# Merged and centred projections, a one-pass gate, and scans handed out in quarter steps in a four-layer image network on one Trainium2 core

## The chip, the core and the metric

The kernel runs on one NeuronCore of a Trainium2 chip. Its engines work side by side, each through its own list of instructions in order: TensorE (PE, matrix products into PSUM), VectorE (DVE, elementwise work and scans), ScalarE (ACT, functions such as the exponential), GpSimd (POOL) and SyncE (SP), which here issues the transfers. The metric is the time on the device in microseconds, the median of several executions. Everything is computed in fp32.

## The reference

Eight images of 256 channels and 32 x 32 pixels (1024 tokens) pass through four layers, each `x = x + layer(group_norm(x))`:

- layer 0: attention with 8 heads of 64, with normalised q and k, then a projection (`wout`);
- layers 1 and 2: a 3x3 convolution of 256 to 256 channels each;
- layer 3: a mixer, of which the change touches nearly every part:

```python
xn = layernorm(xs)                      # over channels, then split in 4 branches of 64
u, z = split(xs @ inw.T)                # per branch, 128 wide each
u = silu(causal depthwise conv of 4 taps (u))
xdbc = u @ xpw.T                        # 4 + 16 + 16 values: dt, B, C
dt = softplus(xdbc[..., :4] @ dtw.T + dtb)
y = selective_scan(u, dt, B, C, -exp(alog), dp)   # h = exp(dt*A)*h + dt*u*B; y = sum(h*C)
xm = y * silu(z) @ outw.T + skip * xc
Q = conv1x1(grouped conv of 3 taps (x_concat, 4 groups)); g = sigmoid(Q); xg = g * xm
R = conv1x1(depthwise3(xg)) + xg
xm2 = conv1x1(depthwise3(concat(xs, R))) + xs
x_local = depthwise3(xm2)
x_global = mha(xm2) = softmax(q k / sqrt(32)) v @ outw.T + outb    # 8 heads of 32
x_out = concat(x_local, x_global) @ fc_w.T + fc_b
x_out = gelu(layernorm(x_out)); xi = ln_hw(x_out)
xi = depthwise 3x3 (xi); x_mixed = layernorm(xi) @ proj_w.T + proj_b
```

## The kernel before, in words

A token row of 1024 values lies along the free dimension, channels on the 128 partitions, so an activation is two tiles of 128 x 1024. A projection from 256 to 256 channels is 2 x 2 x 2 matmuls of 128 x 128 x 512. The profile shows each fp32 matmul as two records.

**Two streams.** For one image the work is cut into `front_attention`, `front_convs` (layers 0 to 2), `scan_layers` (the four branches with their scans), then `back_layers` (gate, the convolutions of layer 3, its attention), `back_out` (the projections `aout` and `fcw`) and `back_end` (layer norm, GELU, 3x3 taps, layer norm, `projw`). The last loop of `preact_stack` (lines 1363 to 1400) works on three images at once: while the scans of image b run, the *dense* stream does the back of image b-1 and the front of image b+1. All are generators. A dense piece yields a cost; `interleave` adds these up and takes one step of the scans for each `PACE[b]` of cost (1.8 for the first image, 2.95, and 1.6 for the last). What is left of the scans is done at the end. `amid` (line 1348) puts pieces of `back_end` among the pieces of `front_convs`, at numbered places; `slow` counts the costs of the front's attention at 0.35. The order on each engine follows this order of issue: the wrapper `Paced` (line 93, whose line 101 is the line of nearly all instructions in the profile) ties each scan instruction to come after the dense instruction issued before it on the same engine, and blocks under `urgent` come early.

**The scans.** `scan_steps` (line 885) has 64 units an image: 4 branches x 2 halves of 512 tokens x 4 quarters of the states x 2 pairs of groups. A unit loads `dt`, `du` and `bc` from DRAM, ScalarE makes two decays `exp(dt*a)` into the two `da` buffers of PSUM, GpSimd makes the drives (`drive`, line 931), DVE scans twice (`tensor_tensor_scan`), GpSimd weighs the result (`weigh`, line 963) and PE sums it over states (`add_up`, into `y`). Before the change a unit takes two steps: both decays, then both scans with `weigh`, `drive` and `add_up`. `branch_front` prepares a branch in six pieces: the product with `minw` into `raw`, the taps and tanh into `u`, the product with `mxpw` into `low` (4 + 16 + 16 rows), then from rows 32 to 35 of `low` the product with `mdtw` and the softplus, then the stores of `dt` and `du`. `branch_back` ends a branch in two pieces. Both take `da` buffers for their products, and `scan_layers` puts their pieces between the steps of the scans.

**The back.** The gate in `back_layers` is a convolution of three taps from 256 to 4 rows: for each tap and channel tile a matmul with 4 columns of weights (12 in all), a copy by ScalarE to `q4`, then a product with `qpr` and a tanh. Attention in layer 3 (`mixer_attention`) leaves its unnormalised output in `o`; the sums go to DRAM and back, are inverted, spread by DMA into `rs`, and `finish` multiplies `o` by `rs` and adds the bias of v. `back_out` projects `o` with `aout` to `glob` and then `local` and `glob` with `fcw` to `xo`, which goes to DRAM; `back_end` loads it again and starts with `layer_norm` (line 293): mean over channels by a matmul with `mean_w`, subtraction, squares, variance, scale.

Of the kernel before, what the change touches and what calls it, by code (L numbers as in the profile page):

```python
# [11 lines left out]
F32 = mybir.dt.float32  # L12
# [21 lines left out]
def preact_stack(ctx: ExitStack, tc: tile.TileContext, I, out, cols):  # L34
# [25 lines left out]
    dp = ctx.enter_context(tc.tile_pool(name="dp", bufs=2, space=DRAM))  # L60
    xdp = ctx.enter_context(tc.tile_pool(name="xdp", bufs=3, space=DRAM))
# [87 lines left out]
    def chunk(name, i):  # L149

        src = I[name]
        k, n = src.shape[2:]
        t = wsp.tile([P, HALF], F32, tag="w", name="w")
        t = t[:, 0 : k * n].rearrange("p (k n) -> p k n", n=n)
        nc.sync.dma_start(out=t, in_=src[i])
        return t
# [4 lines left out]
    mdtw = wp.tile([36, NB, P], F32, name="mdtw")  # L161
    nc.sync.dma_start(out=mdtw[32:36], in_=I["mdtw"])
    qpw = wp.tile([NB, NB], F32, name="qpw")
    nc.sync.dma_start(out=qpw, in_=I["qpw"])
    qdwb = wp.tile([NB, 1], F32, name="qdwb")
    nc.sync.dma_start(out=qdwb, in_=I["qdwb"])
# [25 lines left out]
    qdw = wp.tile([P, 2, 3, NB], F32, name="qdw")  # L192
# [5 lines left out]
    qpr = wp.tile([NB, NB, 64], F32, name="qpr")  # L198
    vector.tensor_copy(qpr, qpw.unsqueeze(2).to_broadcast([NB, NB, 64]))
# [13 lines left out]
    vector.tensor_scalar_mul(qdw, qdw, 2.0)  # L213
    half_d = wp.tile([P, NB], F32, name="half_d")
# [9 lines left out]
    for t in images + [raw]:  # L224
        nc.gpsimd.memset(t, 0.0)

# [66 lines left out]
    def layer_norm(ts, sq, parts, small, finish):  # L293


        for tok, psum in parts:
            pm = psum()
# [418 lines left out]
    def conv3x3(xt, mv, name, bname, evac):  # L716
# [10 lines left out]
        for m in range(2):  # L727
            ps = big_tile()
            n = 0
            for c in range(2):  # L730
                for dy in range(3):
# [11 lines left out]
                    if n < 18:  # L743
                        yield 5.2
            evac(m, ps)
            channel_stats(mv, m, xt[:, m])
            yield 5.2
# [36 lines left out]
    def branch_front(i, xn, br):  # L784
# [3 lines left out]
        for h in range(2):  # L788
            ps = da_tile()
            tensor.matmul(  # L790
                ps,
                minw[rows, j, 0:P],
                inner(xn[j])[rows, HALVES[h]],
                start=True,
                stop=True,
            )
            scalar.copy(raw[:, 3 + h * HALF : 3 + (h + 1) * HALF], ps)
        yield
        u = mp.tile([P, N], F32, tag="u", name="u", bufs=2)
        uu = u[:, 0:N]  # L800
        scalar.activation(
            uu,
            raw[:, 3 : 3 + N],
            AF.Identity,
            bias=col("convb", i),
            scale=col("convw", 4 * i + 3),
        )
        for k in range(3):
            vector.scalar_tensor_tensor(
                uu, raw[:, k : k + N], col("convw", 4 * i + k), uu, ALU.mult, ALU.add  # L810
            )
        th = raw[:, 3 : 3 + N]
        scalar.activation(th, uu, AF.Tanh, scale=0.5)
        vector.scalar_tensor_tensor(uu, th, 1.0, uu, ALU.add, ALU.mult)
        br["u"] = u
        yield

        low = mwork("low")
        for h in range(2):
            ps = da_tile()  # L820
            tensor.matmul(
                ps[0:36], mxpw[:, i], u[:, HALVES[h]], start=True, stop=True
            )
            scalar.copy(low[0:36, HALVES[h]], ps[0:36])
        br["bc"] = dp.tile([DS, 2, 2, HALF], F32, tag="bc", name="bc")
        for k in range(2):
# [3 lines left out]
            )  # L830
        yield

        a, dt = mwork("a"), mwork("dt")
        aa, ee, dd = a[:, 0:N], raw[:, 3 : 3 + N], dt[:, 0:N]
        for h in range(2):
            ps = da_tile()
            tensor.matmul(
                ps, mdtw[32:36, i], low[32:36, HALVES[h]], start=True, stop=True  # L840
            )
            vector.tensor_scalar_add(a[:, HALVES[h]], ps, col("dtb", i))
        scalar.activation(ee, aa, AF.Abs)
        scalar.activation(ee, ee, AF.Exp, scale=-1.0)
        yield
        vector.tensor_scalar_add(dd, ee, 1.0)
        vector.scalar_tensor_tensor(ee, dd, -1.0, ee, ALU.add, ALU.subtract)
        scalar.activation(dd, dd, AF.Ln)
        vector.tensor_sub(dd, dd, ee)
        vector.scalar_tensor_tensor(dd, aa, 0.0, dd, ALU.max, ALU.add)  # L850
        store(br, "dt", dd)
        yield
        vector.tensor_mul(aa, dd, uu)
        store(br, "du", aa)
        yield

    def branch_back(i, xn, br):
# [3 lines left out]
        for h in range(2):  # L861
# [9 lines left out]
            scalar.activation(zh, ps, AF.Tanh, scale=0.5)  # L871
            vector.scalar_tensor_tensor(zh, zh, 1.0, ps, ALU.add, ALU.mult)
        vector.tensor_mul(u[:, 0:N], u[:, 0:N], z[:, 0:N])
        yield
        for h in range(2):
# [7 lines left out]
            )  # L883

    def scan_steps(branches):
# [47 lines left out]
        def decays(u):  # L933
            u["da"] = []
            for e in range(2):
                at = u["i"] * 16 + u["q"] * 4 + 2 * u["gp"] + e
                da = da_tile()
                scalar.activation(
                    da, u["dt"][:, e], AF.Exp, scale=a_neg[:, at : at + 1]
                )  # L940
                u["da"].append(da)

        def scan(u):
            br, hs, q = branches[u["i"]], u["hs"], u["q"]
            if u["h"] == 0 and q == 0 and u["gp"] == 0:
                br["carry"] = sp.tile([P, 4, 4], F32, tag="carry", name="carry")
            for e in range(2):
                g = 2 * u["gp"] + e
                vector.tensor_tensor_scan(
                    hs[:, e],  # L950
                    u["da"][e],
                    hs[:, e],
                    0.0 if u["h"] == 0 else br["carry"][:, q, g : g + 1],
                    ALU.mult,
                    ALU.add,
                )
# [29 lines left out]

        for n in range(-2, len(units) + 2):
            done = None
            for ahead, stage in (
                (2, load), (0, decays), (0, None), (0, scan), (-1, weigh), (1, drive)  # L990
            ):
                if stage is None:
                    yield
                elif 0 <= n + ahead < len(units):
                    stage(units[n + ahead])
# [4 lines left out]
    def scan_layers(img):  # L1000
# [20 lines left out]
        def fronts():  # L1021
            for i in range(1, NB):
                for n, _ in enumerate(branch_front(i, xn, branches[i])):
                    yield 16 * i - 10 + 7 * n // 4

        front, ending, due, n = fronts(), iter(()), 0, 0
        steps = scan_steps(branches)
        while True:
            next(ending, None)
            while due is not None and n >= due:  # L1030
                due = next(front, None)
            if next(steps, END) is END:
                break
            yield
            done = next(steps)
            if done is not None:
                ending = branch_back(done, xn, branches[done])
            n += 1
            yield
        yield from ending  # L1040
# [3 lines left out]
    def mixer_attention(x2, img, exact=False):  # L1044
# [44 lines left out]
        def head(i):  # L1089
            t, rows = i // 4, slice((i % 4) * 32, (i % 4) * 32 + 32)  # L1090

            def take(half, acc):

                vector.tensor_scalar_add(
                    o[t][rows, half], acc, col("ain_b", 4 + t, rows)
                )
# [15 lines left out]
        def pair(i):  # L1112
# [6 lines left out]
            def take(h, acc, _):  # L1119
# [13 lines left out]
                if i % 4 == 2 and h == 1:  # L1133
                    ot = o[t][:, 0:N]

                    def finish(r):
                        vector.tensor_mul(ot, ot, r)
                        vector.tensor_scalar_add(ot, ot, col("ain_b", 4 + t))

                    return invert(sums[t], 4, 32, finish)  # L1140
# [10 lines left out]
    def back_layers(img, exact=False, begin=None):  # L1151
# [5 lines left out]
        for h in range(2):  # L1157
            n = 0
            for j in range(2):
                for k in range(3):  # L1160
                    tensor.matmul(
                        ps[0:NB, HALVES[h]],
# [368 lines left out]
```

## Time and profile before

| | |
|---|---|
| time, median of 3 (lowest to highest) | 6621.78 us (6604.92 to 6635.64) |
| span of the profiled execution, mean granted TensorE clock | 6630.4 us, 0.892 |
| matmul groups: attention values, convolutions | 1189.7 us (4096 records), 1073.7 us (2304) |
| chain that ended last: PE, DVE, DMA, issue | 53%, 25%, 6%, 6% |
| DVE scans | 628.2 + 600.0 us (1024) |
| GpSimd products, `drive` and `weigh` | 1319.8 and 1278.8 us (512 each) |
| decays on ScalarE | 688.7 us (1024) |

Busy time of an engine counts each moment once, so overlapping matmuls are not added. Groups are named output<-inputs with the names of the tiles (`big`, `acc`, `da` and `y` are PSUM buffers). In the row of busy tenths each digit is a fortieth of the span; the row PEclk below it gives the granted clock in the same slices. A wait is written "who <- whom": the engine and tile that stood idle, and what ended the idle time.

### The profile page before, as it was taken

What the parts mean: (1) busy time and instruction counts of PE and PEld (TensorE: products, weight loads), DVE (VectorE), ACT (ScalarE), POOL (GpSimd) and SP (SyncE); (2) the same over time, 40 slices, a digit from 0 to 9 for tenths busy, and PEclk for the clock granted to TensorE, in tenths of its full rate; (3) what the DMA queues carried; (4) which work ended last, traced back from release to release, by engine and by line L of the source; (5) the groups of instructions that cost most, each with busy time, mean ns of one, the idle gap of its engine ahead of it and who ended that gap; (6) DMA issues with size and microseconds to landing.
All of it is one profiled execution on the core that took longest, in us unless ns stands there. A gap on an engine that the chain in (4) does not pass through costs nothing.

```text
span 6630.4 us, 52730 instructions
## 1 busy us (share of the span) xinstructions
PE 5708.6 (86%) x17602; PEld 1926.6 (29%) x17602; DVE 3903.6 (59%) x4613; ACT 2687.2 (41%) x3225; POOL 2684.8 (40%) x1295
## 2 busy tenths in 40 slices
PE   8887689897998979998899989999799988978596
PEld 2331133222422234222332223222342223311222
DVE  4248745577465775567655675557755676455522
ACT  4134424553254532544245432555235442344242
POOL 0016662634355251642526334462526426176300
PEclk9988888998998989899999989899899999867697
DMA  1022332322233122331223222241213212233200
GB/s 41 27 60 79 77 90 73 101 60 65 74 97 91 48 69 76 88 83 52 76 78 92 70 64 80 72 110 45 79 59 105 79 53 80 65 94 89 58 21 26
DMA packets 217969, 471.36 MB, mean 71 GB/s; under 512 B 60244, under 2 KB 103636, under 8 KB 215640
## 3 DMA queue, kind: packets, MB, share of 16 engines
q1 hardware_dynamic: 217688, 467.90, 25.4%
q8 instruction: 141, 2.31, 0.1%
q14 instruction: 140, 1.15, 0.1%
HBM read 395.36 MB, written 63.96 MB: 69 GB/s over the span
## 4 chain that ended last, share of the span: by engine, by line
PE 53%; DVE 25%; DMA 6%; issue 6%; ACT 5%; POOL 4%; SPq 1%; POOLq 0%; DVEq 0%; ACTq 0%
PE big L101 34%; PE acc L101 12%; DVE hs L101 5%; PE da L101 4%; DVE p L101 3%; PE y L101 2%; DVE u L101 2%; DVE dw L101 2%; POOL hs L963 2%; POOL hs L931 2%; DVE t L101 1%; DVE dt L101 1%; DMA du_m<-a 1%; DVE st L101 1%; ACT p L101 1%
## 5 line engine op out<-in xcount | busy, mean ns | idle before, releaser
L931 POOL TENSOR_TENSOR hs<-du,bc 128x1024 f32<-128x1024 f32 x512 | 1319.8, 2594 | 1912.6 <-DMA du<-du_m 767.4
L963 POOL TENSOR_TENSOR hs<-hs,bc 128x1024 f32<-128x1024 f32 x512 | 1278.8, 2498 | 693.2 <-DVE hs L101 480.4
L101 ACT ACTIVATE p<-big 128x1024 f32<-128x1024 f32 x1024 | 1036.1, 1019 | 769.3 <-PE big L101 764.8
L101 PE MATMUL acc<-p,v 128*64 128x512 f32 x4096 | 1189.7, 653 | 2.6 <-ACT o L101 2.6
L101 PE MATMUL big<-im,w 128*128 128x512 f32 x2304 | 1073.7, 622 | 120.9 <-ACT im L101 102.6
L101 ACT ACTIVATE da<-dt,a_neg 128x512 f32<-128x512 f32 x1024 | 688.7, 687 | 791.3 <-DVE hs L101 484.3
L101 DVE TENSOR_TENSOR p<-p 128x1024 f32<-128x1024 f32 x448 | 717.0, 1600 | 273.7 <-ACT p L101 183.9
L101 DVE TENSOR_TENSOR_SCAN hs<-da,carry,hs 128x512 f32<-128x512 f32 x512 | 628.2, 1268 | 382.8 <-POOL hs L931 301.2
L101 DVE TENSOR_TENSOR_SCAN hs<-da,hs 128x512 f32<-128x512 f32 x512 | 600.0, 1207 | 256.8 <-ACT da L101 166.3
L101 PE MATMUL big<-q,k 64*128 64x512 f32 x2048 | 602.5, 657 | 76.7 <-ACT p L101 47.8
L101 PE MATMUL big<-qk,qk 32*128 32x512 f32 x2048 | 658.2, 687 | 9.2 <-ACT p L101 6.5
L101 PEld LDWEIGHTS big<-im,w 128*128 128x128 f32 x2304 | 445.4, 198 | 752.0 <-issue 613.8
L101 PE MATMUL y<-hs,sel 128*32 128x512 f32 x2048 | 410.9, 676 | 210.9 <-POOL hs L963 180.8
L962 POOL COPY carry<-hs 128x2 f32<-128x2 f32 x256 | 97.5, 381 | 947.6 <-DVE hs L101 928.2
L101 PEld LDWEIGHTS acc<-p,v 128*64 128x64 f32 x4096 | 217.6, 140 | 843.2 <-issue 759.8
L101 PEld LDWEIGHTS big<-qk,qk 32*128 32x128 f32 x2048 | 173.8, 195 | 487.2 <-issue 269.2
L101 PEld LDWEIGHTS big<-q,k 64*128 64x128 f32 x2048 | 161.2, 188 | 503.0 <-issue 247.4
L101 PE MATMUL big<-o,w 128*128 128x512 f32 x384 | 196.2, 664 | 92.6 <-DVE o L101 92.6
L101 PE MATMUL big<-xn,w 128*128 128x512 f32 x512 | 232.4, 608 | 5.6 <-ACT p L101 5.6
L101 DVE SCALAR_TENSOR_TENSOR dw<-xo,vec,dw 128x961 f32<-128x961 f32 (+1 forms) x128 | 194.1, 1550 | 29.3 <-ACT dw L101 29.1
L101 DVE SCALAR_TENSOR_TENSOR u<-raw,vec,u 128x1024 f32<-128x1024 f32 x96 | 153.9, 1603 | 87.2 <-ACT u L101 86.7
L101 DVE SCALAR_TENSOR_TENSOR xt<-big,vec,xt 128x1024 f32<-128x1024 f32 x48 | 61.4, 1279 | 236.2 <-PE big L101 236.2
(191 smaller groups left out, 5231.1 us busy)
## 6 DMA issues: line engine op xcount, KB each, us to landing
bc<-bc SPq DMA_DIRECT2D x1024, 128.0 KB
dt<-dt_m SPq DMA_DIRECT2D x512, 128.0 KB
du<-du_m SPq DMA_DIRECT2D x512, 128.0 KB
w<-in_wc SPq DMA_DIRECT2D x192, 192.0 KB
rs<-inv SPq DMA_DIRECT2D x64, 256.0 KB
dt_m<-dt SPq DMA_DIRECT2D x64, 256.0 KB
du_m<-a SPq DMA_DIRECT2D x64, 256.0 KB
xt<-in_x SPq DMA_DIRECT2D x8, 1024.0 KB
```

The source lines that it names most:

```text
L101: made = issue(*args, **kwargs)
L931: nc.gpsimd.tensor_mul(u["hs"], u["du"], both_groups(u["bc"][:, 0]))
L962: nc.gpsimd.tensor_copy(carry[:, u["q"], g : g + 2], hs[:, :, HALF - 1])
L963: nc.gpsimd.tensor_mul(hs, hs, both_groups(u["bc"][:, 1]))
```

## The change

1. **Merged projections.** The output projection of the attention is folded into the one after it: `fc_w[:, global] @ aout` is computed once by `merge_weights` on the chip, during the first front, and kept in DRAM. So `fcw` reads `local` and `o` directly and `aout` is gone. The bias of v moves through both products into `fc_b`, so `finish` only multiplies.
2. **Centred last projection.** The mean over output channels is taken out of the merged weights and of `fc_b`, so `xo` has mean zero and the first layer norm of `back_end` starts with the squares (`centred=True`).
3. **Gate in one pass.** The three taps stand side by side in the columns of `qdw` (3 x 32), so that 4 matmuls make all taps at once; three copies by ScalarE, each shifted by a token, put them on 96 rows of `q4`, and the product with `qpr` adds them up.
4. **Delta without the low-rank detour.** `mdtw` is made once as the product of the two weights, so `dt` comes from `u` in one product; `low` has only B and C.
5. **Quarter steps.** A scan unit takes four steps (decay, decay, scan with `weigh` and `drive`, scan with `add_up`), `PACE` becomes 0.9, 1.37 and 0.74 a step; `branch_front` and `branch_back` yield after each operation; the taps in `back_end` yield one by one, a convolution after each column of taps; and `amid` places the pieces of `back_end` by cost spent instead of by number. This is for spreading the scan work more evenly between the dense pieces.

```diff
-        src = I[name]
+        src = fc_w if name == "fcw" else I[name]
...
-    mdtw = wp.tile([36, NB, P], F32, name="mdtw")
-    nc.sync.dma_start(out=mdtw[32:36], in_=I["mdtw"])
+    mdtw = wp.tile([P, NB, P], F32, name="mdtw")
...
+            if centred:
+                for t in range(2):
+                    scalar.activation(sq[t][:, tok], ts[t][:, tok], AF.Square)
+                continue
...
+        def at(n, stage, *args):
+            if 0 <= n < len(units):
+                stage(units[n], *args)
+
         for n in range(-2, len(units) + 2):
+            at(n + 2, load)
+            at(n, decay, 0)
+            yield
+            at(n, decay, 1)
+            yield
+            at(n - 1, weigh)
+            at(n + 1, drive)
+            at(n, scan, 0)
+            yield
+            at(n, scan, 1)
             done = None
-            for ahead, stage in (
-                (2, load), (0, decays), (0, None), (0, scan), (-1, weigh), (1, drive)
-            ):
-                if stage is None:
-                    yield
-                elif 0 <= n + ahead < len(units):
-                    stage(units[n + ahead])
...
-                    yield 16 * i - 10 + 7 * n // 4
+                    yield 64 * i - 42 + 2 * n
...
-        front, ending, due, n = fronts(), iter(()), 0, 0
-        steps = scan_steps(branches)
-        while True:
-            next(ending, None)
-            while due is not None and n >= due:
-                due = next(front, None)
-            if next(steps, END) is END:
-                break
-            yield
-            done = next(steps)
+        front, ending, due = fronts(), iter(()), 0
+        for n, done in enumerate(scan_steps(branches)):
             if done is not None:
                 ending = branch_back(done, xn, branches[done])
-            n += 1
             yield
+            next(ending, None)
+            if due is not None and n >= due:
+                due = next(front, None)
...
             for j in range(2):
-                for k in range(3):
-                    tensor.matmul(
-                        ps[0:NB, HALVES[h]],
-                        qdw[:, j, k],
-                        xm[j][:, k + h * HALF : k + (h + 1) * HALF],
...
+                tensor.matmul(
+                    ps[0:96, HALVES[h]],
+                    qdw[:, j].rearrange("p k n -> p (k n)"),
+                    inner(xm[j])[:, HALVES[h]],
...
-        scalar.activation(q4[0:NB, 0:N], ps[0:NB], AF.Identity, bias=qdwb)
-        yield 10
...
+            rows = slice(k * 32, k * 32 + 32)
+            scalar.activation(
+                q4[rows, to], ps[rows, at], AF.Identity, bias=qdwb[rows]
+            )
+        yield 4
...
-        yield from project_both("aout", o, evac_glob)
...
-        yield from project_both("fcw", local + glob, evac_fc)
+        srcs = [t[:, 0:N] for t in local + o]
+        yield from project_both("fcw", srcs, evac_fc)
...
-        yield from layer_norm(xo, sq, WHOLE, acc_tile, affine("lgn_w", "lgn_b", AF.Gelu))
+        yield from layer_norm(xo, sq, WHOLE, acc_tile, affine("lgn_w", "lgn_b", AF.Gelu), True)
...
-                if n % 2:
-                    yield 1
+                yield 0.5
...
-    PACE = [1.8] + [2.95] * (batch - 2) + [1.6]
+
+    ENDS = [74, 77, 88, 99, 114]
+    PACE = [0.9] + [1.37] * (batch - 2) + [0.74]
...
             yield from islice(front, 4)
-            ending = back_out(last)
-            yield from islice(ending, 2)
             yield next(front)
-            yield from ending
+            yield from back_out(last)
...
-                (0, 4, 6, 7, 8, 9, 10, 11, 12, 13, 14, 16, 17, 20, 22, 25),
+                [0, 13.7, 20] + [23 + 2.7 * k for k in range(16)] + ENDS,
```

## The prediction

> **What bounds the kernel now.** I read the page first: the busy shares, then the busy tenths of TensorE (PE) and the clock that it was granted.
>
> ```profile
> PE 5708.6 (86%) x17602; PEld 1926.6 (29%) x17602; DVE 3903.6 (59%) x4613; ACT 2687.2 (41%) x3225; POOL 2684.8 (40%) x1295
> PE   8887689897998979998899989999799988978596
> PEclk9988888998998989899999989899899999867697
> ```
>
> PE is the only engine near full; the next, VectorE (DVE), has 59%. The page gives no stages, so I cut the span where the gate of each image is applied (`gate` on ScalarE) and asked for PE alone in these stretches. The six middle stretches last 767.9 to 781.8 us; one of them and the second last are:
>
> ```profile
> 3357.20:4135.50 778.30, 693.26 (x2201) 0.92 0.27 76
> 5685.20:6312.90 627.70, 469.37 (x1221) 0.72 0.28 76
> ```
>
> Columns: stretch, length, PE busy, granted clock, DMA share, GB/s. In a middle stretch PE is busy for 693 of 778 us, and the missing clock costs more: PE is short of work for 85 us. A wait costs twice, since work after it runs at a lower clock. In the stretch from 5685 us PE is far less full. What PE waits for in the middle stretch (columns: total us, times, longest):
>
> ```profile
> PE y L101 <- POOL hs L963: 18.7, 6, 7.0
> PE big L101 <- ACT im L101: 13.8, 2, 10.5
> PE big L101 <- DVE o L101: 9.8, 2, 8.5
> PE da L101 <- DVE hs L101: 7.5, 3, 4.4
> PE y L101 <- DVE u L101: 5.0, 1, 5.0
> ```
>
> and in 5760 to 6312 us:
>
> ```profile
> PE y L101 <- POOL hs L963: 54.9, 19, 7.5
> PE da L101 <- DVE hs L101: 25.7, 9, 7.4
> PE big L101 <- DVE o L101: 13.0, 1, 13.0
> PE da L101 <- DVE u L101: 8.7, 2, 6.7
> ```
>
> Two kinds stand out: scan work that PE meets before it is ready (`y`, `da`), and `o`, the attention output that waits for its division by the softmax sums. The timeline of PE around that second wait:
>
> ```profile
> 3640.59 3.70 PE L101 MATMUL big<-o,w 128*128 128x512 f32 x8
> 3652.84 6.60 PE L101 MATMUL big<-o,w 128*128 128x512 f32 x8 [8.55 <-DVE o L101]
> 3659.28 7.03 PE L101 MATMUL big<-xn,w 128*128 128x512 f32 x16
> ```
>
> This is the projection `aout`: its first source is ready, its second is not. Every fp32 matmul of the program shows as two records ("passes"): the gate has 12 matmuls an image and 24 records. A pass of 512 columns takes 0.44 us at full clock (16 in 7.03 us).
>
> **The Trainium skill.** "TensorE: Matmul & The Clock Gate", Part 1 (the clock gate), says that an idle window of some 3.4 us drops the clock to half. The trace agrees: after 8.55 us idle, eight passes took 6.60 us instead of 3.70. The same page, architectural detail, says that matmuls stay in order and only weight loads are pulled ahead; so here, where nothing overtook the wait on `o`. "Perfetto Trace Analysis", Optimizing Scalar/DVE Operations, says that splitting instructions can help where Vector or Scalar work, unsaturated, leaves gaps elsewhere. That bears on the quarter steps, and this trace shows the disease:
>
> ```profile
> 3957.74 5.57 DVE L101 SCALAR_TENSOR_TENSOR dw<-xo,vec,dw 128x961 f32<-128x961 f32 x3
> 3961.19 1.92 PE L101 MATMUL y<-hs,sel 128*32 128x512 f32 x4 [7.01 <-POOL hs L963]
> ```
>
> The DVE lines are taps that run in a block ahead of a scan; GpSimd, which weighs the scan, and PE, which sums it, come late.
>
> **The change, part by part.**
>
> *Merged projections.* `aout` goes, folded into `fcw`: 16 passes fewer an image. In the middle stretch the spot from 3640.59 to 3659.28 us, 18.7 us with wait and half clock, drops out. The wait does not come back: `fcw` now reads `o`, but after the 16 passes of the next image's first q and k (7.0 us) and its own 16 on `local` (7.1 us). PE then wants the second `o` at least 14 us after 3640.6, and it was there at 3652.8, sooner without the bias addition (0.75 us on DVE). 6 x 18.7 = 112 us. In the stretch from 5685 us no other front lies between; PE met `o` at 6161.5, then ran 6.7 us on it, waited 7.6 us for the weights of `fcw` and had 10.6 us of its passes to do which now come ahead of `o`: some 20 us allowing for a remaining wait. In the tail `aout` starts at 6498.9 and `fcw` ends at 6531.6. After: 24 ready passes take 10.6 us, `o` is ready at about 6512, eight more passes take 3.5 us: 6515.6, a gain of 16. Sum 148 us. The copies of `glob` (17.8 us of ScalarE) and the bias additions (26.5 us of DVE) also go; costed at nothing, since PE's work hides them.
>
> *Centred projection.* The first layer norm of `back_end` loses its mean: eight passes and two subtractions an image.
>
> ```profile
> L101 PE MATMUL big<-xo,mean_w 128*128 128x512 f32 x64 | 35.6, 701 | 11.7 <-DMA xo<-xo_d 11.7
> ```
>
> 3.6 us in six middle stretches (the subtractions lie under the convolution), and 8 us each in the last stretch with scans (passes at half clock) and in the tail, where squares can start when `xo` lands at 6537.5 instead of 6545.5. 22 + 16 = 38 us.
>
> *Gate in one pass.* 24 passes become 8: 10.5 us to 3.5.
>
> ```profile
> 3340.55 10.46 PE L101 MATMUL big<-xn,qdw 128*4 128x512 f32 x24
> 3352.29 4.62 PE L101 MATMUL big<-q,qpr 4*128 4x512 f32 x8
> ```
>
> Against it, one copy of 1.10 us becomes three on ScalarE. Behind the three stand the `qpr` matmuls and behind these the whole of PE's row; the statistics of the next scans, also in line here, gain. 7.0 - 2.2 = 4.8 us, eight times: 38 us.
>
> *Setup, once.* 20 passes of one column at 0.22 us (111.4/512), 8 of 256 columns at 0.23 (57.7/256), 8 of 128 at 0.15 (38.0/256): 7.4 us. PE also meets some waits: DVE between dependent columns (0.65 us each, as in the group norm) and loads. One load round trip in the tail left PE idle for 5.9 us. Bounds 7 and 25 us; I take 14. The four added small loads ahead of x are issued in 0.3 us each and lie in it.
>
> *Delta without the low-rank detour.* `mdtw` multiplies `u` at once: the same number of passes; only a chain gets shorter, which other work covers. Nothing.
>
> *Quarter steps, one operation at a time.* No work is removed. The dense costs that the code yields in a middle stretch add up to 459 before for 147 half steps at 2.95, and to 446 after for about 300 quarter steps at 1.37; the scans still end at 92% (before 94%). A scan unit takes 5.48 of dense cost instead of 5.9: 7% tighter. GpSimd's two products of 2.6 and 2.5 us a unit are far below the 10 us that a unit takes. What finer steps can take away is the waits of PE on scan work: 18.7 + 7.5 + 5.0 = 31.2 us in a middle stretch, 89.3 in 5760 to 6312 us (above), and by the same view 27.5 + 14.1 + 6.5 = 48.1 us in 460 to 1023. Sum 6 x 31.2 + 89.3 + 48.1 = 325 us. New waits come with it: fronts and ends take `da` buffers (two) between the two decays, so that the second decay waits on ScalarE for the first scan. Behind it stand the exponentials of attention, and PE's value matmuls wait for those. The before trace has no such order. Lower bound: all new waits cancel the gain (0). Upper: half of the 325 goes, 162. I take a quarter, 81.
>
> Sum: -148 - 38 - 38 + 14 - 81 = -291 us, 6622 - 291 = **6331 us**.
>
> **Rivals.**
> A. *The finer steps move waits without removing them*: the waits on the division and the passes go, and 6622 - 210 = 6412 us remain. For it: 7% tighter pace, the `da` buffers. Against: blocks of taps and of front work visibly delay scans.
> B. *Half of the scan waits go or more*, with the clock higher afterwards: 6250. For it: the 0.72 clock and 89 us of waits near the end. Against: many waits come from GpSimd behind DVE, which a different order only shortens.
> C. *The shared `da` buffers become the bound*: each scan unit's second decay late, exponentials behind it, PE starved through attention. If the 325 us of scan waits double, 6412 + 325 = 6737, slower than before. Against: ScalarE is busy 43% of a middle stretch, and most quarter steps take no extra `da`.
> D. *The gain is given back to within 0.5%*: the same, with 65% of that loss, about 6620.
>
> **How the numbers follow.** Forecast 0.45, A 0.22, B 0.22, C 0.07, D 0.04. The range takes in the forecast, most of A and most of B, with setup at its bounds: 6200 to 6500. Faster 0.89 (forecast, A, B), same 0.04 (D), slower 0.07 (C).
>
> **What would show it.** PE's records fall by 40 an image (320) before the setup's are added. No `aout` spot, and no wait of PE on `o` above 2 us in a middle stretch; `qdw` 8 passes in 3.5 us; no `xo` mean. Middle stretches of 735 to 750 us (778 - 27, less a quarter of 31). PE's waits on `y` and `da` in a middle stretch near 23 us; if they are 31, A holds; if ScalarE's decays wait long on `hs` and PE on `p`, C. I am wrong if `o` still makes PE wait after `local`, or if the stretch shrinks by less than 20 us.

## The result: slightly slower, and the profile after

The changed kernel took 6666.12 us (median of 4, 6663.18 to 6830.99), the kernel before 6617.29 us on the same chip: ratio 1.0072, 95% interval 1.0046 to 1.0097. The forecast was 6331 us; the time lies above its range of 6200 to 6500 us, on the side of rival C, but without the doubled scan waits that made C. The profiled execution below is the one of 6831 us: in it the last attention ran wholly at half clock, 114 us longer than in the kernel before, and the other executions, of 6663 to 6669 us, are shorter by more than 160 us, so only what recurs in the middle stretches is read from it as the loss, with its size taken from the medians.

The page of the changed kernel, its first row:

```profile
PE 5842.5 (86%) x17318; PEld 1925.6 (28%) x17318; DVE 3824.2 (56%) x4611; ACT 2681.0 (39%) x3225; POOL 2684.1 (39%) x1297
```

PE has 284 records fewer (320 gone, the setup's added) and yet was busy 134 us longer, 113 of them in the last attention: not more work, but work at a lower clock. The same two stretches, from gate to gate, PE alone (stretch, length, PE busy, clock, DMA share, GB/s):

```profile
3432.30:4227.40 795.10, 706.32 (x2161) 0.88 0.26 74
5800.70:6414.30 613.60, 434.82 (x1185) 0.74 0.28 77
```

The middle stretch grew from 778 to 795 us, though PE has 40 records fewer in it. Its idle time is 88.8 us (85.0 before). What PE waits for has changed its names (us in total, times, longest):

```profile
PE big L102 <- ACT p L102: 18.1, 7, 5.3
PE da L102 <- DVE u L102: 10.2, 1, 10.2
PE acc L102 <- DVE mv L102: 9.6, 1, 9.6
PE y L102 <- POOL hs L981: 9.1, 4, 4.3
PE da L102 <- DVE hs L102: 8.9, 6, 3.5
PE big L102 <- ACT im L102: 8.2, 2, 6.8
```

`o` is gone from the list and `y` fell from 18.7 to 9.1 us. In their place stand `p` (attention's exponentials, 4.3 us before), `u` and `mv`. The scan lines in the second-last stretch (5875 to 6414 us, again from 75 us after the gate):

```profile
PE y L102 <- POOL hs L981: 80.4, 31, 12.8
PE da L102 <- DVE hs L102: 24.2, 10, 4.7
```

Scan waits are 104.6 us here, and 108.5 with the 3.9 us on `u`, against 89.3 before: more, not fewer. The finer steps need not be the reason, for a kernel below with the old half steps has 105.5 us there.

The parts that remove work did so. Where the `aout` spot was, the timeline of PE now shows the projections without a gap on `o`:

```profile
3759.56 7.13 PE L102 MATMUL big<-local,w 128*128 128x512 f32 x16
3766.53 3.60 PE L102 MATMUL big<-o,w 128*128 128x512 f32 x8
...
3772.55 3.70 PE L102 MATMUL big<-o,w 128*128 128x512 f32 x8
```

and the gate is 8 passes of 3.60 us and one wait of 2.28 us on `q`; from its first matmul to the `qpr` product 7.0 us pass (11.7 before):

```profile
3422.54 3.60 PE L102 MATMUL big<-xn,qdw 128*96 128x512 f32 x8
...
3429.56 2.50 PE L102 MATMUL big<-q,qpr 96*128 96x512 f32 x4 [2.28 <-ACT q L102]
```

To see where the gain went I cut the fourth of the image stretches (before from 3357 us, after from 3432 us) at the first and last matmul of each kind; the right three columns belong to experiments below (us):

| | before | after | before, 64 rows | after, 64 rows | parts alone, 64 rows |
|---|---|---|---|---|---|
| gate to q and k | 71 | 69 | 71 | 69 | 73 |
| mixer attention | 189 | **226** | 179 | 191 | 185 |
| v, `fcw` | 67 | 49 | 67 | 49 | 53 |
| front attention | 176 | 174 | 175 | 174 | 190 |
| `wout` to convolution | 59 | 52 | 60 | 52 | 50 |
| convolution 1 | 119 | **134** | 122 | 134 | 134 |
| convolution 2 | 98 | 90 | 98 | 92 | 93 |

Two rows took the gain: the mixer's attention (+37 us) and the first convolution (+15 us). In the attention the timeline of PE shows how it begins:

```profile
3502.67 1.13 PE L102 MATMUL big<-qk,qk 32*128 32x512 f32 x4 [0.32 <-DVE qk L102]
3507.73 2.08 PE L102 MATMUL big<-qk,qk 32*128 32x512 f32 x4 [3.93 <-ACT p L102]
3509.73 1.98 PE L102 MATMUL acc<-p,v 128*64 128x512 f32 x4
```

After a gap of 3.93 us the same four passes take 2.08 instead of 1.13 us. The gap comes from ScalarE, which stood 17 us for the first `dt` of the image and then made two decays before the first exponential:

```profile
3504.14 1.28 ACT L102 ACT_TABLE_LOAD   x1 [17.01 <-DMA dt<-dt_m]
3505.43 1.30 ACT L102 ACTIVATE da<-dt,a_neg 128x512 f32<-128x512 f32 x2
3506.67 1.92 ACT L102 ACTIVATE p<-big 128x1024 f32<-128x1024 f32 x2
```

The kernel before has the same order, but there `dt` landed 69.5 us after the gate (71.8 here) and the first scores began 70.7 us after it (68.9 here), so its decays ran beside the first scores and no such gap arose. And PE stays slow for long (same columns as above):

```profile
3506.00:3584.50 78.50, 71.45 (x142) 0.50 0.27 67
3584.50:3663.00 78.50, 73.91 (x294) 1.00 0.39 104
```

PE is busy 71 of 78.5 us and the clock stays at 0.50; in the next 78.5 us, as busy, it does 294 records instead of 142. The tail, where no scan runs beside the attention, shows it barest: before and after,

```profile
6366.80:6495.70 128.90, 128.58 (x501) 1.00 0.05 13
```

```profile
6469.10:6712.40 243.30, 241.97 (x499) 0.51 0.02 6
```

The same matmuls, PE idle for 1.3 us in all, nearly twice the time. The half clock began behind a gap of 1.0 us, and idleness is not what kept it. The scores are matmuls on 32 rows of weights (`32*128`), two heads at a time: 64 of 128 rows of the array. The front attention, with 64 rows a head, stays at 0.99 (before, 3684 to 3860 us). That became the theory to test.

### The profile page after: what moved, and what is told of

The parts are those of the page before. It is cut to its first block, busy times and chain, and to the rows that moved or that the text cites. A ratio compares the mean times of both kernels' runs of the same rounds, so it can differ in the third digit from the quotient of the medians.

```text
span 6829.2 us, 52021 instructions
## 1 busy us (share of the span) xinstructions
PE 5842.5 (86%) x17318; PEld 1925.6 (28%) x17318; DVE 3824.2 (56%) x4611; ACT 2681.0 (39%) x3225; POOL 2684.1 (39%) x1297
## 3 DMA queue, kind: packets, MB, share of 16 engines
q8 instruction: 139, 2.28, 0.1%
## 5 line engine op out<-in xcount | busy, mean ns | idle before, releaser
L102 PE MATMUL acc<-p,v 128*64 128x512 f32 x4096 | 1307.4, 712 | 11.2 <-ACT o L102 5.5
L102 PE MATMUL big<-qk,qk 32*128 32x512 f32 x2048 | 803.8, 824 | 108.7 <-ACT p L102 106.0
L102 DVE TENSOR_TENSOR p<-p 128x1024 f32<-128x1024 f32 x448 | 691.0, 1543 | 263.7 <-ACT p L102 187.4
L980 POOL COPY carry<-hs 128x2 f32<-128x2 f32 x256 | 116.2, 454 | 1064.9 <-DVE hs L102 1051.4
L102 PEld LDWEIGHTS big<-qk,qk 32*128 32x128 f32 x2048 | 203.6, 229 | 704.0 <-ACT p L102 331.1
L102 PE MATMUL da<-xn,w_minw 64*128 64x512 f32 x256 | 164.1, 731 | 54.2 <-DVE hs L102 54.1
```

Source lines behind the costliest of these rows:

```text
L102: made = issue(*args, **kwargs)
L980: nc.gpsimd.tensor_copy(carry[:, u["q"], g : g + 2], hs[:, :, HALF - 1])
```

## The experiments

**Theory**: a pause of some microseconds drops TensorE to half clock, and the mixer's attention, on 32-row scores, does not bring it back until full-array matmuls pass; the change makes such pauses. **Rival**: the quarter steps or the added waits slow the attention themselves, and the clock only follows.

**Later scans.** Eight empty quarter steps after the first front, so that the first decays come later than the first exponentials:

```diff
         for _ in branch_front(0, xn, branches[0]):
             yield
+        for _ in range(8):
+            yield
```

> The changed kernel with eight empty scan steps between the first branch's preparation and the first scan unit of each image, so that the first decays are issued after the mixer attention has begun. Theory L (latch): in each middle stretch PE idles 3.93 us at the start of the mixer attention, because the first decays, which wait on ScalarE for the transfer of dt, stand ahead of the first exponentials; the clock falls to half and attention alone does not bring it back for some 78 us, which costs 39 us. Then the long low-clock episode goes and the time falls by 6 x 20 to 6 x 39 us, to 6430 to 6545. Rival Q (quarter steps): the decays and scans dealt out in small pieces delay exponentials all through the attention, and the low clock only follows. Then moving the start changes less than 30 us: 6635 to 6690.

6678.99 us, ratio 1.0074 (1.0052 to 1.0096): nothing gained. The gap at the attention's start is gone, but another, of 3.24 us, came 25 us later, before a branch's first matmul, which waited for `hs`, with 23.9 us of half clock behind it, and three more episodes followed, none of them behind a gap above 1.5 us. The longest, 30.7 us, began at 3640.0 us after PE had been busy without a gap for more than 10 us: an episode needs no pause. The mixer attention took 189 to 220 us. One episode is replaced by the next.

**Keeper.** Three pairs of extra full matmuls with the identity, early in the mixer attention; their result is not used:

```diff
+            if keep is not None and n in (3, 5, 7):
+                s = big_tile()
+                for e in range(2):
+                    tensor.matmul(s[:, HALVES[e]], ident, keep[:, HALVES[e]], start=True, stop=True)
```

> The changed kernel with two more full-array matmuls (128 x 128 x 512, result unused) at the attention steps 3, 5 and 7 of each mixer attention; 5.3 us of PE work an image at full clock, 42 in all. Theory L says that what ends a low-clock episode is work on the whole array, which the mixer attention (32 rows of weights) lacks: the episode ends some 20 us after the start instead of 78, which saves about 29 us a middle stretch, 175 in all, less 42 added: 6530. If whole-array work does not end the episode, the 42 us are added: 6706.

6669.52 us, ratio 1.0064 (1.0042 to 1.0086). The timeline of PE in the fourth image:

```profile
3480.87 2.07 PE L102 MATMUL big<-qk,qk 32*128 32x512 f32 x4 [4.13 <-ACT p L102]
...
3488.69 3.78 PE L102 MATMUL big<-x,ident 128*128 128x512 f32 x4
3492.40 1.17 PE L102 MATMUL big<-qk,qk 32*128 32x512 f32 x4
```

The gap is there, 4.13 us, and the first pair of 128-row matmuls ends the half clock: scores take 2.07 us before it and 1.17 us after it. The episode shrank from 78.5 to 13.7 us. The whole did not gain: the three pairs cost 5.3 us an image at full clock (estimated as 12 passes of 0.44 us), a gap of 6.0 us came after the last pair with 27.3 us of half clock, and others remained. It shows what ends an episode, not yet what they cost.

**Parts alone, steps alone.** The first takes items 1 to 3 of the change with the half steps of before; the second takes items 4 and 5 on the kernel before.

> The kernel before with the merged and centred projections and the gate in one pass, but with its own half steps, pace, places and preparation of branches. If the sum of the prediction for the parts holds and no new low-clock episode comes: 6617 - 210 = 6407. If the earlier start of the mixer attention alone brings the wait for dt (theory L with the parts as its cause): a long episode shows in the middle stretches and the time is 6560 to 6650. Theory Q: 6407.

> The changed kernel with its projections, layer norm and gate put back as before, so that only the quarter steps, pace, places and the direct delta remain. Theory Q: the steps cost what the parts gain and more, 6664 + 210 = 6874, with exponentials waiting through the attention. Theory L: the attention starts some 2 to 5 us later again relative to dt, the gap falls under the length that drops the clock, and the time is 6560 to 6680.

6787.1 us, ratio 1.025 (1.0218 to 1.0281), and 6991.95 us, 1.0535 (1.0473 to 1.0598). Each half alone is far worse than both together, and worse than any time that had been expected of it. The parts alone take 15 us off v and `fcw` and lose 30 in the mixer attention (219 us).

**64 rows.** Scores over two heads' rows in one product, in the changed kernel and in the kernel before. Counts and shapes of all else stay; the scores mix two heads:

```diff
-                "q": [qk[t][r, 0:N] for r in rows],
-                "k": [qk[2 + t][r, 0:N] for r in rows],
+                "q": [qk[t][e * 64 : e * 64 + 64, 0:N] for e in range(2)],
+                "k": [qk[2 + t][e * 64 : e * 64 + 64, 0:N] for e in range(2)],
```

> The changed kernel with the scores of the mixer attention taken over 64 rows of q and k instead of 32, in the same number of matmuls of the same length; the scores of two neighbouring heads are then added, so the output differs from the reference, the work on every other engine does not. Theory L, made sharper by the first runs: in the mixer attention the array works on 64 of 128 rows, which is so near the activity at which the clock is granted that a bubble of one to four us drops it to half for 10 to 80 us. With 128 rows (as in the front attention, whose clock is 0.97 to 1.00) the clock stays up: mixer attention 170 to 185 us instead of some 220 in a middle stretch, 6664 - 6 x 40 - some 30 in the last scan stretch: about 6390. If waits on scans and exponentials, not the clock, set the time of the attention: within 30 us of 6664.

> The same edit in the kernel before: scores over 64 rows, two neighbouring heads added, the output differs for that reason. Theory L: its mixer attention has 19 us of low-clock loss in a middle stretch and more in the last scan stretch: 6617 - 6 x 17 - 30 = about 6485, and the changed kernel with this edit is then 80 to 150 us faster than this one, as the parts of the prediction without scan waits would have it. Rival: within 30 us of 6617.

6490.15 us, ratio 0.9794 (0.9778 to 0.9811), and 6575.59 us, 0.9921 (0.9904 to 0.9937). The same gap stands at the same place in the changed kernel, and costs only the next matmuls:

```profile
3397.21 2.08 PE L102 MATMUL big<-qk,qk 64*128 64x512 f32 x4 [3.92 <-ACT p L102]
3399.21 1.97 PE L102 MATMUL acc<-p,v 128*64 128x512 f32 x4
3401.11 1.76 PE L102 MATMUL big<-qk,qk 64*128 64x512 f32 x4
3402.80 1.08 PE L102 MATMUL acc<-p,v 128*64 128x512 f32 x4
```

6.8 us of half clock instead of 78.5, and the whole is 176 us shorter. This decides for the theory: no wait and no step was changed. The clock granted in the executions that were not profiled agrees: 0.871 to 0.874 in the four of the changed kernel of 6663 to 6669 us, 0.903 to 0.905 with 64 rows; 0.890 to 0.897 in the kernel before, 0.904 to 0.908 with 64 rows. The rival keeps a share: of the 37 us by which the mixer attention grew, 12 stay with 64 rows in both kernels (191 against 179).

**64 rows, true scores.** The two heads of a pair are taken from two different 64-row blocks, and the query tile exists twice, each with the other heads' rows multiplied by zero, so that the output is the reference's (two more DVE operations an image):

```diff
+                qk[t] = [qk[t], work("qk3")]
+                for r in range(2):
+                    vector.tensor_scalar(
+                        qk[t][r][:, 0:N], ps, col("ain_b", t), odd[:, r : r + 1], ALU.add, ALU.mult
+                    )
...
-            rows = [slice((j % 4) * 32, (j % 4) * 32 + 32) for j in (i, i + 1)]
+            rows = [slice((j % 4) * 32, (j % 4) * 32 + 32) for j in (i, i + 2)]
+            wide = [slice(e * 64, e * 64 + 64) for e in range(2)]
...
-                "q": [qk[t][r, 0:N] for r in rows],
-                "k": [qk[2 + t][r, 0:N] for r in rows],
+                "q": [qk[t][r][w, 0:N] for w in wide],
+                "k": [qk[2 + t][w, 0:N] for w in wide],
```

> The changed kernel with scores over 64 rows and the reference's result: q is written twice, each time with the other heads' rows set to zero by a per-partition factor, heads are paired 0 with 2 and 1 with 3, so that both 64-row groups work at once. Two more copies of 1.28 us on VectorE an image and two more tiles out of the twelve work buffers. Theory L: the gain of the 64 rows less some us for the copies and fewer free buffers: 6390 to 6450. If zeros in half of the rows count as idle, no gain: 6665 to 6700.

6486.59 us, ratio 0.9794 (0.9776 to 0.9812), as with the mixed scores. It beats both kernels. Half of the query rows are zeros and the time is the same: the rows in use count here, not the zeros that flow through them.

> The changed kernel itself, for its timeline beside the others: 6660 to 6670, low-clock episodes of 70 to 80 us at the start of the mixer attention in most middle stretches, the tail's attention near 129 us at full clock.

The changed kernel once more gave 6826.03 us, where 6660 to 6670 had been expected, again with the last attention at half clock behind a gap of 1.0 us.

**Parts and steps apart, with the clock kept up.** The same two halves, the parts with the zeroed rows, the steps with the mixed scores:

> The parts alone (projections, centring, gate) on the half steps of before, with the 64-row scores that keep the reference's result. Two earlier runs leave this open: with 32 rows the parts alone cost 166 us, with 64 rows the whole change gains 85 us over the kernel before with the same edit (6490 against 6576). Theory L: the loss of the parts alone was the clock; here they gain what the prediction's sum says or nearly, 6576 - 210 plus some us for the copies: 6370 to 6450. If the parts hurt the schedule in another way: 6520 or more.

> The steps alone (quarter steps, pace, places, direct delta) with 64-row scores, neighbouring heads added, so the output differs. With the clock kept up, the price of the steps themselves: by the stretches of the whole change, 9 us in the mixer attention and 10 to 14 us in the first convolution of each middle stretch: 6576 + 6 x 20 + 20 = about 6715. If the quarter steps are no loss without the clock: 6550 to 6600.

6579.98 us, ratio 0.994 (0.9923 to 0.9956), and 6800.53 us, 1.0268 (1.0251 to 1.0286). As ratios to the kernel before:

| | 32 rows | 64 rows |
|---|---|---|
| before | 1 | 0.992 |
| parts alone | 1.025 | 0.994 |
| steps alone | 1.0535 | 1.027 |
| both (the change) | 1.007 | 0.979 |

Read downwards in the right column: with most of the attention's half clock gone, the parts alone gain nothing, the steps alone cost 3.5%, both together gain 1.3%. The parts alone are in the table of stretches: v and `fcw` -14, `wout` -10 and convolution 2 -5 us, given back in the front attention (+15), the first convolution (+12) and the mixer attention (+6). There PE meets other things unready; in that kernel:

```profile
3697.09 3.75 PE L102 MATMUL big<-xn,w 128*128 128x512 f32 x4 [4.86 <-DMA w<-in_wqk]
```

```profile
3995.01 3.78 PE L102 MATMUL da<-xn,w_minw 64*128 64x512 f32 x4 [7.84 <-DVE hs L102]
```

weights that have not landed and a scan result that is not there. The steps alone, with 64 rows, did take scan waits away: 19.7 us in the fourth image against 29.5 in the kernel before with 64 rows. But the stretch grew from 772 to 808 us, PE idle for 111 us instead of 85: waits on `p` rose from 3.9 to 14.6 us, and one of 11.2 us on the weights of a convolution came new. Why these came was not settled.

**A pause in the kernel before**, with 32 and with 64 rows: sixteen copies of a small tile in front of the fifth exponential.

> The kernel before with a pause: sixteen small copies on ScalarE (256 columns, some 0.35 us each by the fit of its 512 and 1024 column rows, 5 to 6 us together) ahead of the fifth exponential of each of the eight mixer attentions, so that PE idles there for some 4 to 5 us. Theory L: beside the eight pauses (40 us) each drops the clock to half for 15 to 80 us in the six middle stretches and for all of the tail's attention: 6620 + 40 + 6 x 20 + 110 = about 6890. If a pause costs what it lasts: 6660.

> The same pause in the kernel before with 64-row scores (neighbouring heads added, the output differs). Theory L: the clock is back within two windows of some 3.4 us, so each pause costs its length and some 3 us: 6576 + 40 + 25 = about 6640, and the tail's attention stays near 135 us. If the number of rows does not matter, as much is lost as in the pause run with 32 rows.

6627.87 us, ratio 1.0011 (0.9998 to 1.0024), and 6591.0 us, 0.9943 (0.9915 to 0.997): these runs decide nothing. The copies depend on nothing and were placed where ScalarE had nothing to do, all before 78 us, as the view of that tile shows, so they made no pause:

```profile
L101 ACT ACTIVATE idle<-idle x128: 399/416/420, 3.0 to 77.2; 128x256 f32<-128x256 f32 x128
```

**The same pause by a true dependency.** Five copies of the score tile onto itself ahead of one exponential of each mixer attention, in the kernel before and in its 64-row form:

```diff
+            if not add_up and u["n"] == 4:
+                for _ in range(5):
+                    scalar.activation(s, s, AF.Copy)
             p = work("p")[:, 0:N]
             scalar.activation(p, s, AF.Exp)
```

> The kernel before, with one thing added: in each of the eight mixer attentions five copies of a score tile onto itself (ScalarE, near 1.0 us each, as the exponentials of that tile size take in the trace of before) ahead of the fifth exponential, so that TensorE runs out of work for some 3 to 5 us a few units after the attention's start; nothing else differs, the output is the same. Theory 1 (a pause of some us drops TensorE to half clock, and matmuls on 64 of the 128 rows do not bring it back): the last attention, which has no scans beside it, goes from 129 us to about 230 to 245, the middle attentions from 189 to about 205 to 225 each, the whole to about 6850 (6780 to 6950). Theory 2 (the quarter steps or the decays' order slow the attention by themselves, the clock only shows it): five microseconds in each of eight attentions, so the last one 134 and the whole 6660 (6650 to 6675).

> The same five copies in the kernel before with the scores taken over 64 rows instead of 32 (two heads' rows in one product, so the scores are not the reference's; shapes, instruction counts and output type as before). Theory 1: with all 128 rows of the array at work the clock comes back within some 7 us of each pause, so the last attention is 129 + 5 + about 3 = 137 us and the whole about 6576 + 60 = 6640 (6615 to 6660), some 200 us under the run with 32 rows. Theory 1b (any pause is followed by half clock until the attention ends, whatever the rows): the last attention 230 to 245 here too, the whole near 6800. Theory 2: 6576 + 40 = 6616, and the run with 32 rows only 50 above it.

6754.03 us, ratio 1.0171 (1.0145 to 1.0197), and 6606.68 us, 0.9956 (0.9937 to 0.9975). PE in the last attention, 32 rows:

```profile
6412.78 1.08 PE L101 MATMUL acc<-p,v 128*64 128x512 f32 x4
6417.15 2.08 PE L101 MATMUL big<-qk,qk 32*128 32x512 f32 x4 [3.29 <-ACT p L101]
6419.16 1.98 PE L101 MATMUL acc<-p,v 128*64 128x512 f32 x4
```

64 rows:

```profile
6347.88 2.08 PE L101 MATMUL big<-qk,qk 64*128 64x512 f32 x4 [3.30 <-ACT p L101]
6349.89 1.97 PE L101 MATMUL acc<-p,v 128*64 128x512 f32 x4
6351.79 2.06 PE L101 MATMUL big<-qk,qk 64*128 64x512 f32 x4
6353.78 1.08 PE L101 MATMUL acc<-p,v 128*64 128x512 f32 x4
```

and the attention as a whole, 32 rows and then 64:

```profile
6403.30:6641.30 238.00, 234.38 (x500) 0.53 0.03 7
```

```profile
6333.90:6469.10 135.20, 131.59 (x501) 0.97 0.05 13
```

One gap of 3.3 us, the same in both: with 32 rows it cost 109 us, with 64 rows 6. Nothing of the change is in these kernels. In the middle stretches my numbers were too high: the 32-row attention mostly stayed at 186 to 189 us (once 204) instead of 205 to 225, because scans and fronts put matmuls on all 128 rows behind the gap, and the half clock after it lasted 20.5 us in the fourth image. So a gap costs what it takes until enough of such work comes by; in the changed kernel only 16 `y` passes (5.8 us) and two on 64 rows came between 3511 and 3577 us, and the half clock ended when the projections with `mdtw`, on 128 rows, came at 3577 and 3583 us. The work need not use all columns at once: in the run with later scans the 23.9 us ended under eight `y` passes (`128*32`, from 3538.4 us). Nor is it the value matmuls that hold the clock down. At the end of the changed kernel's last attention twelve of them ran alone, and the clock was full from 6717.9 us on:

```profile
6713.41 5.02 PE L102 MATMUL acc<-p,v 128*64 128x512 f32 x12
```

It is the scores, on half of the rows.

**A later end of the branch.** On the version with true 64-row scores, three more quarter steps between `u * z` on DVE and the projections that read it:

```diff
         vector.tensor_mul(u[:, 0:N], u[:, 0:N], z[:, 0:N])
-        yield
+        for _ in range(4):
+            yield
```

> The changed kernel with scores over 64 rows, half of them zeros (as in the earlier run of 6487 us), and with one more edit: in branch_back three more quarter steps are let pass between the product u times z on VectorE and the two output projections that read it, so that TensorE does not reach them 10 us ahead of VectorE. Theory 1 (this wait of 10.2 us in the first convolution of six stages and its like is a loss of its own on the path): about 40 to 60 us less, 6430 to 6450. Theory 2 (the convolutions are bound by what VectorE and GpSimd still owe to the scans, and the wait only moves to the next reader, as it did in the run with the parts alone): 6475 to 6495, no change beyond 0.2%.

6472.7 us, ratio 0.9748 (0.9727 to 0.9769), 0.5% better than the same kernel without the edit, each against the kernel before on its own chip (the bare times differ by 14 us, on two chips); the intervals lie just apart. The wait only shrank, from 10.2 to 8.03 us, and the next one grew from 0.33 us:

```profile
3912.44 1.97 PE L102 MATMUL da<-u,w_moutw 128*64 128x512 f32 x2 [8.03 <-DVE u L102]
3916.82 1.97 PE L102 MATMUL da<-u,w_moutw 128*64 128x512 f32 x2 [2.42 <-DVE hs L102]
```

The first convolution still takes 134 us. So theory 2 is nearer, though more changed than its 0.2%: the record speaks for DVE's backlog at that place as what holds PE, rather than the position of one reader. It is the fastest version tried, with the reference's output, 2.5% below the kernel before.

## Why the prediction was wrong

- **Merged projections** (-148): right at their place. V and `fcw` lost 18 us in the middle stretches, as the 18.7 us spot said; the part from the last scores to the next gate lost 23 us beside the last scans, where 20 here and 8 for the centring were forecast. In the tail the part from the last scores to the end went from 134 us to between 111 and 114 in the versions with 64 rows, against 24 forecast for both. In the middle stretches PE waits on `o` no more.
- **Gate** (-38): right at its place, 11.7 to 7.0 us, 4.7 where 4.8 was said. The **centred** passes went too.
- **Each saving taken for a saving of the whole, without asking who takes it back** (part of the -148, -38 and -38): the sum from `wout` to the end of convolution 2 was 276 us before and is 276 after, although 3.6 us of means and 4.7 us of gate left it. Where I wrote that work lies under the convolution and costs nothing, DVE's order there sets PE's waits: `u` for 10.2 us, `mv` for 9.6.
- **Quarter steps** (-81, a quarter of 325 us of scan waits): this step failed. By the same sum the changed kernel has 322 us of scan waits (6 x 28.2, 108.5 and 44.6). And the bound was wrong that new waits could at most cancel the gain: the steps alone, with 64 rows, took a third of a middle stretch's scan waits away and made the kernel 225 us slower (6576 to 6801). The timeline of DVE at the wait on `u` shows how the work now stands:

```profile
4062.11 2.43 DVE L102 SCALAR_TENSOR_TENSOR dw<-xo,vec,dw 128x961 f32<-128x961 f32 x1
4064.45 0.67 DVE L102 SCALAR_TENSOR_TENSOR z<-z,da 128x512 f32<-128x512 f32 x1
4065.05 2.73 DVE L102 SCALAR_TENSOR_TENSOR dw<-xo,vec,dw 128x992 f32<-128x992 f32 x1
4067.71 3.35 DVE L102 TENSOR_TENSOR u<-u,z 128x1024 f32<-128x1024 f32 x1
```

  The block of taps ahead of a scan is broken up, as intended, and a wait like that of 7.01 us before is gone. But a tap stands before each link of the chain z, `u * z`, projection, as one did in the kernel before (2.04 us of `dw` between z and `u * z`), and PE now reaches the projection so far ahead of DVE that it waits 10.2 us for it, where it waited 4.4; before, then after:

```profile
3988.01 3.67 PE L101 MATMUL da<-u,w_moutw 128*64 128x512 f32 x4 [4.38 <-DVE hs L101]
```

```profile
4071.12 1.97 PE L102 MATMUL da<-u,w_moutw 128*64 128x512 f32 x2 [10.17 <-DVE u L102]
```

  In a middle stretch scan waits fell only from 31.2 to 28.2 us (forecast 23), and in the second last they rose from 89.3 to 108.5.
- **What I did not price at all: the clock in the attention.** I had the pieces: the page states the clock of each stretch, I wrote that a wait costs twice, and I named decays ahead of exponentials, with PE's value matmuls behind them. I took them as waits of some us in rival C, whose sum came from doubled scan waits. They came as waits of 4 to 5 us (`p`, 18.1 us in a stretch), and behind them PE stayed at half clock until matmuls on all 128 rows filled some microseconds. With 64-row scores the change gains 1.3%, with 32-row scores it loses 0.7%: the clock under the 32-row scores costs the changed kernel some 176 us (6666 to 6490) and the kernel before 51 (6627 to 6576).
- The sum: 335 us lie between forecast and time. Some 125 are the clock (176 - 51). Of the remaining 210, 81 are the quarter steps' gain that never came; of the rest the largest terms are the first convolution, 12 to 15 us in six stretches, and the mixer attention with 64 rows, 9 to 13 us in six. The five middle stretches from 1800 us on agree in both terms. The cause of these two stays open: the order of DVE is seen in the waits and was tried apart only by the one edit above, and the first convolution takes 134 us with the parts alone too.
- **Setup** (+14): the time to the first gate rose from 1024 to 1041 us, though gate and scans were to take 17 off it there. With the parts alone, but no `mdtw` product, it is 1027, and with the whole change but later scans (the first experiment) 1017: so the rest comes from when the scans run, not from the work added.

The Trainium skill, "TensorE: Matmul & The Clock Gate", Part 1, says that the clock is full again after one busy window of some 3.4 us. With 64-row scores the runs agree: of the 6.8 us at half clock (6346.9 to 6353.7 us in the last attention) the first 1.0 us still belong to the gap, and the second 3.4 us are wholly busy. With 32-row scores they differ: 234 us of busy matmuls in 238 us did not do it. The section on HAM oscillation there asks for no idle gap above about 3.4 us; here 3.29 us were enough, in the changed kernel's last attention 1.0 us, and one episode of 30.7 us had no gap ahead of it. (That matmuls stay in order, which the prediction takes from this page, stands in its Part 2.)

## What to carry to other kernels

Before pricing a new wait of TensorE, ask which matmuls stand behind it: if many of them use half of the array's rows, as here, the wait may be paid not once or twice but until some microseconds of matmuls on all rows come by, up to the whole stage. Widening the contraction with zero rows cost nothing in passes here, and the clock came back in 6.8 us in the last attention and in 10.2 to 13.7 us behind most of the same holds in the middle ones. And work taken out of one stage of a row that several engines feed need not be a gain if the next stage's inputs come no earlier; look for its weights and for the slower engine's backlog first.

## What was not expected of the hardware

- The granted clock in these records is 1.0 or 0.5, never between; a stretch's 0.74 is a share of time. Half clock lasts 3.4 us or a multiple of it (6.8, 13.7, 20.5, 23.9, 78.5).
- Attention with scores of 32 rows of weights and values of 64 columns, back to back, stays at half clock for at least 228 us and, if begun at full clock, at full clock for 129 us: there both states held themselves. An estimate from its passes fits this: 2.08 us of scores on half of the rows and 1.98 us of values on all make 74% of the rows in use, at either clock. But beside scans the full clock was also lost without a gap (30.7 us from 3640.0 us in the run with later scans). With 64 rows it returns in 6.8 us, and with half of the query rows zero the time is the same.
- A single gap of 3.29 us, made by five copies on another engine, lengthened a stage of 129 us by 109 us; the same gap with 64-row scores cost 6 us.
